# First group's rows of the last eight batches copied inside SBUF by GpSimd's transfers

## The chip, the cores and the metric

The kernel runs on one core of one Trainium2 chip. The metric is the device time of one execution in microseconds (us), as the median of several runs. Everything is in float32. TensorE is called PE below, VectorE DVE, ScalarE ACT, GpSimd POOL and SyncE SP, as the profile calls them. SP and ACT issue transfers on hardware queues (q1 is SP's and q10 ACT's in the profile), and GpSimd on a software queue (q0).

## The reference

Two residual layers act on x of shape (64, 128, 2048): batch, channel, time. The first multiplies each batch by one of 16 matrices, picked by the batch's token. The second is a long convolution along time with a kernel K that is built for each channel from 64 complex exponentials, plus a skip gain D, masked by each batch's length.

```python
x = x + einsum('bct,bcd->bdt', x, W[token])              # W: (16, 128, 128)

dt  = exp(log_dt); A = -exp(log_A_real) + 1j * A_imag    # per channel h, mode n
dtA = A * dt[:, None]
Ct  = (C[..., 0] + 1j * C[..., 1]) * (exp(dtA) - 1) / A
K   = 2 * einsum('hn,hnl->hl', Ct, exp(dtA[:, :, None] * arange(2048))).real
y   = irfft(rfft(x, 4096) * rfft(K, 4096))[..., :2048] + x * D[:, None]
x   = x + y * (arange(2048)[None, :] < length[:, None])[:, None, :]
```

## The kernel before

**Two layers, two layouts.** Time is cut into two segments of 1024 steps. For segment 0 the kernel first does layer one for all 64 batches, one after the other (`batch0(b)`): channels lie on the partitions, the batch's matrix (with the identity added) is the stationary operand, and the result goes back into the loaded tile and from there to a DRAM scratch `scr[0]`. The second layer wants the batches on the partitions: it works on 32 groups of four channels, and `load(i)` fetches group i as a tile `x_i` of 128 rows (64 batches times two halves of the segment), four channels and 512 steps. So the scratch is a transposition between the layers, and `load(0)` can't start until the last batch has been stored.

**A batch of layer one.** `fetch` (L434 to 438) loads two batches, 1 MB, on SP. `weigh` (L440 to 452) lets GpSimd read the token and copy the matrix into one of four buffers `w1`; batch b + 3's is made when batch b is recorded. `project` (L456 to 467) does four matmuls, evicts both PSUM banks into the tile (ACT from batch 18 on) and lets ACT issue the store into the scratch. Batches 12 to 63 are interleaved with the tables of the convolution; the last of these steps, `store_lags`, sends two small transfers `kpad<-krow` from GpSimd at every second batch up to batch 60.

**The seam.** After batch 63 the kernel records `load(0)`, `load(1)` and `some(8)`: the first eight pieces (half batches, two matmuls each) of layer one for segment 1. These need four matrices from GpSimd and the first two of the segment-1 tiles that `fetches(FILL)` asked for at batch 60. Then comes `iteration(-1)`: it loads `x_2`, fetches the fifth segment-1 tile, and for group 0 does the transposes `turn(0, n)`, the input matmuls, and the DVE scan. From then on one iteration per group follows, with pieces of segment 1's layer one between. Here (s, b) is batch b of segment s.

**Order and waits.** Instructions of an engine run in the order in which they were recorded. All tiles `xb` and `x` share one ring of ten buffers (`big`), handed out in the order of the allocations. A transfer is counted on one of eight counters of its kind: one set of eight for the transfers of SP and ACT together, handed out in turn, and another for GpSimd's. A transfer waits until the one that used its counter before has landed, and an engine that waits to issue a transfer does nothing else meanwhile.

Of the kernel before, what the change touches and what calls it, by code (L numbers as in the profile page):

```python
# [41 lines left out]
F32 = mybir.dt.float32  # L42
# [6 lines left out]
P = 128  # L49
# [322 lines left out]
def cond_resid_ssm_kernel(  # L372
# [13 lines left out]
    nc = tc.nc  # L386
    ctx.enter_context(tc.manual_schedule())
    B, C, L = x.shape
# [4 lines left out]
    HL = SL // 2  # L393
    KK = HL // Q
    NQ = 2 * KK
    BK = 512
# [3 lines left out]
    CG = 2 * GP  # L400
# [11 lines left out]
    big = ctx.enter_context(tc.tile_pool(name="big", bufs=10))  # L412
    s0 = ctx.enter_context(tc.tile_pool(name="s0", bufs=4))
    dram = ctx.enter_context(tc.tile_pool(name="dram", bufs=1, space=DRAM))
    psp = ctx.enter_context(tc.tile_pool(name="psp", bufs=1, space=PSUM))

    scr = [dram.tile([P, C, HL], F32, tag=f"scr{s}", name=f"scr{s}") for s in range(NS)]
# [10 lines left out]
    xbs, w1s = {}, {}  # L428
    BT = 2
    QB = SL // BK  # L430
# [3 lines left out]
    def fetch(s, n):  # L434

        xbs[s, n] = big.tile([P, BT, SL], F32, tag="x", name=f"xb_{s}_{n}")
        src = x[n * BT : (n + 1) * BT, :, s * SL : (s + 1) * SL]
        nc.sync.dma_start(xbs[s, n], src.rearrange("b c t -> c b t"))

    def weigh(s, b, plus=None):  # L440

        w1s[s, b] = s0.tile([P, C], F32, tag="w1", name=f"w1_{s}_{b}")
        at = nc.values_load(
            ci[:, b : b + 1],
            engines=(mybir.EngineType.Pool,),
            min_val=0,
            max_val=S - 1,
            skip_runtime_bounds_check_because="it is clamped above",
        )
        w = wres[:, bass.ds(at, 1), :].rearrange("p s d -> p (s d)")  # L450
        if plus is None:
            nc.gpsimd.tensor_copy(w1s[s, b], w)  # L452
        else:
            nc.gpsimd.tensor_tensor(w1s[s, b], w, plus, ALU.add)

    def project(s, b, q, ps, n_banks=1, copy=nc.scalar.copy):  # L456

        n, r = divmod(b, BT)
        own = xbs[s, n][:, r, :]
        for k in range(n_banks):  # L460
            cols = slice((q + k) * BK, (q + k + 1) * BK)
            nc.tensor.matmul(ps[:, k], w1s[s, b], own[:, cols], start=True, stop=True)  # L462
        cols = slice(q * BK, (q + n_banks) * BK)
        copy(own[:, cols], ps.rearrange("p k t -> p (k t)"))  # L464
        if q + n_banks == QB:
            to = scr[s].rearrange("(f b) c t -> b c f t", f=2)[b]
            nc.scalar.dma_start(to, own.rearrange("c (f t) -> c f t", f=2))
            del w1s[s, b]
            if r == BT - 1:
                del xbs[s, n]  # L470

    def batch0(b, copy=nc.scalar.copy):
        if b % BT == 0 and b // BT + AHEAD < B // BT:
            fetch(0, b // BT + AHEAD)
        if b + WAHEAD < B:
            weigh(0, b + WAHEAD)
        project(0, b, 0, psp.tile([P, QB, BK], F32, tag="y", name=f"p0_0_{b}", bufs=2), QB, copy)

    V = nc.vector
    es = [tab.tile([P, TP, 2, NE], F32, tag=f"e{g}", name=f"e_{g}") for g in range(NT)]  # L480
# [4 lines left out]
    def exps(g):  # L485

        for i in range(TP):
            nc.scalar.activation(es[g][:, i, 0, :], steps, AF.Exp, scale=par_of(DRE, g, i))
# [12 lines left out]
    with tc.tile_pool(name="setup", bufs=1) as setup:  # L501
# [87 lines left out]
        for b in range(3):  # L589
            batch0(b)  # L590
        par.sines()
        run(others)
        batch0(3)
        par.lay("ppar_1", rows, 3, par.row(gtab, DRE))
        run(par.gains())
        phases = _weave(par.phases(), masks(), par.steps_of_chunk())
        for b in range(4, 10):
            batch0(b)
            run(phases, 12)
            if b >= 6:  # L600
                exps(b - 6)
# [20 lines left out]
    def partial_angles(k):  # L622

        own = parts[:, :, 0:NL]
        by_l = some_l.unsqueeze(1).to_broadcast([P, NP, NL])

        def of(row, n):
            return gtab[:, row, :].unsqueeze(2).to_broadcast([P, NP, n])

        if k == 0:  # L630
            V.tensor_tensor(own, of(FHI, NL), by_l, ALU.mult)
        elif k == 1:
            V.tensor_scalar(whole, own, MAGIC, MAGIC, ALU.add, ALU.subtract)
        elif k == 2:
            V.tensor_tensor(own, own, whole, ALU.subtract)
        elif k == 3:
            V.tensor_tensor(whole, of(FLO, NL), by_l, ALU.mult)
        elif k == 4:
            V.tensor_tensor(own, own, whole, ALU.add)
        else:  # L640
            V.tensor_tensor(parts[:, :, 0:8], parts[:, :, 0:8], of(PHI, 8), ALU.add)
            V.tensor_tensor(parts[:, :, 24:25], parts[:, :, 24:25], of(PHI, 1), ALU.add)
            V.tensor_scalar(last, parts[:, :, 24:25], MAGIC, MAGIC, ALU.add, ALU.subtract)
            V.tensor_tensor(last, parts[:, :, 24:25], last, ALU.subtract)
# [76 lines left out]
    def some(n):  # L721
        nonlocal done
        for s, b, q in pieces[done : done + n]:
            weights_for(done + WAHEAD * QB + 1)
            project(s, b, q, psp.tile([P, 1, BK], F32, tag="tr", name=f"p0_{s}_{b}_{q}", bufs=2))
            done += 1

    def fetches(n):

        nonlocal begun  # L730
        while begun < min(n + BT * QB, len(pieces)):
            fetch(pieces[begun][0], pieces[begun][1] // BT)
            begun += BT * QB
# [5 lines left out]
            told += QB  # L739

    ps = {}
    FIRST = 18
# [10 lines left out]
        0: turn_parts,  # L755
    }
    for now in range(12, B):
        batch0(now, V.tensor_copy if now < 18 else nc.scalar.copy)
        if now < 20:

            by_row = d_in.rearrange("(h j c d) -> c d j h", j=8, c=2, d=2)
            with nc.allow_non_contiguous_dma(reason="128 gains, four times"):
                for i, r in ((i, r) for i in range(TP) for r in range(4) if (i * 4 + r) // 2 == now - 12):
                    nc.gpsimd.dma_start(dcol[i * NR + r : (i + 1) * NR : 4, :], by_row[r % 2, r // 2])
        if now == 21:
            V.tensor_scalar(dcol, dcol, 1.0, None, ALU.add)
        if now < FIRST:
            partial_angles(now - 12)
        if now < 18:
            exps(2 * now - 20)  # L770
            exps(2 * now - 19)
        for lag, step in STEPS.items():
            g, odd = divmod(now - FIRST - lag, 2)
            if not odd and 0 <= g < NT:
                step(g)
        if now == 60:
            fetches(FILL)
    assert not ps and not ts and not ks
    tmp.__exit__(None, None, None)
    early.__exit__(None, None, None)  # L780


    s1 = ctx.enter_context(tc.tile_pool(name="s1", bufs=2))
    xs, us, ss, bts, tts, ys = {}, {}, {}, {}, {}, {}
    half = [slice(0, B), slice(B, P)]
    NI = NS * NG

    def seg(i):
        return divmod(i, NG)

    def load(i):
        s, g = seg(i)
        xs[i] = big.tile([P, CG, HL], F32, tag="x", name=f"x_{i}")
        nc.sync.dma_start(xs[i], scr[s][:, g * CG : (g + 1) * CG, :])
# [70 lines left out]
    def scan(i, lo, hi):  # L865

        s, g = seg(i)
        st = ss[i]

        def times(row, new, src, own, d):  # L870
            pair = g * GP + d
            factor = ptab[:, row, pair : pair + 1]
            nc.vector.scalar_tensor_tensor(new[:, d, 0:2], src, factor, own[:, d, 0:2], ALU.mult, ALU.add)  # L873

        for m in range(max(lo, 1 if s == 0 else 0), min(hi, NQ if s < NS - 1 else NQ - 1)):
            f, k = divmod(m, KK)
            old, own = st[:, :, :, k, f, :], st[:, :, :, k + 1, f, :]
            new = st[:, :, :, 0, 1, :] if m == KK - 1 else own
            for d in range(GP):
                times(LR, new, old[:, d, 0:2], own, d)  # L880
                if d == 0:
                    nc.vector.tensor_scalar(old[:, :, 2], old[:, :, 0], -1.0, None, ALU.mult)  # L882
            for d in range(GP):
                times(LI, new, old[:, d, 1:3], new, d)
# [49 lines left out]
    def iteration(i):  # L934
# [35 lines left out]
                scan(i + 1, 2, 3) if seg(i + 1)[0] == 0 else scan(i + 1, 1, 2)  # L970
        if nxt:
            scan(i + 1, 3 if seg(i + 1)[0] == 0 else 2, NQ)
    load(0)
    load(1)
    some(8)
    for i in range(-1, NI):
# [33 lines left out]
```

## Time and profile before

| | |
|---|---|
| time, median of 3 runs | 1125.23 us (1122.19 to 1125.81) |
| the profiled execution's own time | 1122.48 us |
| its span | 1120.7 us |
| busy: PE, weight loads, DVE, ACT, POOL | 96%, 70%, 72%, 61%, 22% of the span |
| batches 0 to 63 of segment 0 end on PE at | about 180 us |
| groups of the convolution begin at | 192.1 us |

The page divides the span by engine; the chain of waits gives the work that ended last, from the start to the end; a timeline lists single instructions with their start, their length and, in brackets, how long the engine had idled and for whom. Transfers have two times: what the issuing engine spent, in the timeline, and the time from the issue to the landing, in the list of transfers. About 180 us of 1120 lie before the seam, some 12 us around it; the rest is the loop over the groups, which in its steady part takes 16.55 us a group (the first output matmuls of two consecutive groups start at 217.66 and 234.22 us).

### The profile page before, as it was taken

Reading aid. Unit: us, or ns where it says so; the run is one execution under the profiler, and the core shown is the slowest. Engines: PE = TensorE matmul, PEld = TensorE weight load, DVE = VectorE, ACT = ScalarE, POOL = GpSimd, SP = SyncE. Lnnn points to the kernel's source line nnn. Section 1 sums busy time; section 2 is a strip of 40 time slices with the busy share of each in tenths; the row PEclk is TensorE's granted clock in tenths of the full one; section 3 lists DMA queues with packets and bytes.
Section 4 is the critical chain, followed back from the end, with each engine's and each line's share of the span. In section 5 each row is a group of like instructions: output and inputs, shape, how many; then the busy total and the mean of one; then the engine's idle time right before and its main releaser. Section 6 shows DMA issues by size and latency. Waiting matters only on the chain.

```text
span 1120.7 us, 23853 instructions
## 1 busy us (share of the span) xinstructions
PE 1076.6 (96%) x8634; PEld 786.6 (70%) x8634; DVE 803.0 (72%) x2671; ACT 680.7 (61%) x1123; POOL 242.5 (22%) x421
## 2 busy tenths in 40 slices
PE   5779998999999999999999999999999999999996
PEld 2224443677777777777777778888888888888885
DVE  7656550467657667667666758888888888888886
ACT  3577665766666566566566566665566566556652
POOL 3253332121221212122122211211211111121110
PEclk9899999999999999999999999999999999999999
DMA  9999999999999999999999887787787887788754
GB/s 346 415 398 386 409 410 379 357 281 285 344 280 294 298 293 298 302 299 281 293 299 284 260 264 212 225 228 226 229 228 210 237 230 223 216 240 228 210 166 118
DMA packets 117126, 313.25 MB, mean 280 GB/s; under 512 B 11858, under 2 KB 11986, under 8 KB 108818
## 3 DMA queue, kind: packets, MB, share of 16 engines
q1 hardware_dynamic: 70928, 218.65, 62.1%
q10 hardware_dynamic: 35106, 67.64, 16.1%
q0 software_dynamic: 10976, 25.45, 8.9%
q8 instruction: 68, 1.11, 0.4%
q14 instruction: 48, 0.39, 0.1%
HBM read 164.76 MB, written 146.93 MB: 278 GB/s over the span
## 4 chain that ended last, share of the span: by engine, by line
PE 91%; DMA 3%; DVE 2%; ACT 1%; issue 1%; ACTq 0%; SPq 0%; POOLq 0%; DVEq 0%
PE y L911 21%; PE y L899 20%; PE v L858 18%; PE p L462 17%; PE tr L833 10%; DMA xb<-in_x_dram 2%; PE pb L815 2%; PE pt L660 1%; DMA scr<-xb 1%; PE pk L690 1%; DVE s L873 1%; DMA x<-scr 1%; ACT xb L464 0%; DVE xb L464 0%; DVE x L920 0%
## 5 line engine op out<-in xcount | busy, mean ns | idle before, releaser
L873 DVE SCALAR_TENSOR_TENSOR s<-s,ptab 128x128 f32<-128x128 f32 x1792 | 520.2, 343 | 109.0 <-ACT s L863 92.7
L863 ACT ACTIVATE s<-v,ptab 64x512 f32<-64x512 f32 (+1 forms) x512 | 336.0, 656 | 50.4 <-PE v L858 33.9
L899 PEld LDWEIGHTS y<-tt,u 128*128 128x128 f32 x2048 | 263.5, 192 | 80.5 <-issue 67.0
L462 PE MATMUL p<-xb,w 128*128 128x512 f32 x512 | 257.9, 617 | 22.4 <-DMA xb<-in_x_dram 10.9
L899 PE MATMUL y<-tt,u 128*128 128x128 f32 x2048 | 269.9, 275 | 0.1
L911 PEld LDWEIGHTS y<-e,s 64*128 64x128 f32 x4096 | 233.9, 188 | 46.6 <-issue 24.2
L858 PE MATMUL v<-u,bt 128*128 128x512 f32 (+1 forms) x512 | 248.6, 567 | 0.0
L911 PE MATMUL y<-e,s 64*128 64x128 f32 x4096 | 246.7, 275 | 1.4 <-DVE s L873 1.4
L834 ACT COPY u<-tr 128x512 f32<-128x512 f32 x256 | 150.5, 588 | 156.6 <-PE tr L833 130.2
L882 DVE TENSOR_SCALAR s<-s 128x128 f32<-128x128 f32 x448 | 98.8, 221 | 137.6 <-ACT s L863 137.6
L464 ACT COPY xb<-p 128x512 f32<-128x512 f32 (+1 forms) x186 | 133.4, 718 | 83.9 <-PE p L462 80.7
L920 DVE COPY_PREDICATED x<-mask,y 128x1024 f32<-128x1024 uint8 x128 | 166.5, 1301 | 1.1 <-PE y L911 1.0
L833 PEld LDWEIGHTS tr<-ident,x 128*128 128x128 f32 x1024 | 121.6, 141 | 54.8 <-issue 49.3
L833 PE MATMUL tr<-ident,x 128*128 128x128 f32 x1024 | 156.3, 275 | 3.9 <-DMA x<-scr 3.9
L462 PEld LDWEIGHTS p<-xb,w 128*128 128x128 f32 x512 | 87.9, 197 | 89.3 <-issue 80.1
L452 POOL COPY w<-wres 128x128 f32 x125 | 58.6, 469 | 291.7 <-PE p L462 291.3
L801 POOL DMA_DIRECT2D tt<-kpad x64 | 50.5, 789 | 207.3 <-DVE s L873 168.0
L858 PEld LDWEIGHTS v<-u,bt 128*128 128x128 f32 x512 | 79.9, 192 | 13.9 <-issue 13.6
L846 POOL DMA_DIRECT2D s<-carry x64 | 44.9, 706 | 126.1 <-PE y L911 121.4
L816 ACT COPY bt<-pb 128x512 f32<-128x512 f32 x32 | 18.8, 586 | 87.5 <-PE pb L815 86.7
L890 POOL DMA_DIRECT2D carry<-s x64 | 43.6, 721 | 69.7 <-DVE s L873 63.6
L843 POOL MEMSET s<- 128x384 f32 x32 | 14.8, 462 | 149.4 <-DMA carry<-s 66.6
(199 smaller groups left out, 296.1 us busy)
## 6 DMA issues: line engine op xcount, KB each, us to landing
xb<-in_x_dram SPq DMA_DIRECT2D x64, 1024.0 KB, 10.1
scr<-xb ACTq DMA_DIRECT2D x128, 512.0 KB, 8.3
x<-scr SPq DMA_DIRECT2D x64, 1024.0 KB, 8.1
out_dram<-x SPq DMA_DIRECT2D x126, 512.0 KB, 4.8
tt<-kpad POOLq DMA_DIRECT2D x64, 256.0 KB, 5.9
btd<-bt SPq DMA_DIRECT2D x32, 256.0 KB, 7.2
bt<-btd SPq DMA_DIRECT2D x32, 256.0 KB, 4.9
carry<-s POOLq DMA_DIRECT2D x64, 64.0 KB, 7.1
```

The costliest lines, as they stand in the source:

```text
L452: nc.gpsimd.tensor_copy(w1s[s, b], w)
L462: nc.tensor.matmul(ps[:, k], w1s[s, b], own[:, cols], start=True, stop=True)
L464: copy(own[:, cols], ps.rearrange("p k t -> p (k t)"))
L833: nc.tensor.transpose(tr[:, k, :], xs[i][:, c, k * Q : (k + 1) * Q], ident)
L834: nc.scalar.copy(u, tr)
L858: nc.tensor.matmul(v[:, 0:nv], w, us[i, n].rearrange("p k r -> p (k r)")[:, 0:nv], start=True, stop=True)
L863: nc.scalar.activation(own[:, 0:nv], v[lanes, 0:nv], AF.Copy, scale=amp)
L873: nc.vector.scalar_tensor_tensor(new[:, d, 0:2], src, factor, own[:, d, 0:2], ALU.mult, ALU.add)
L882: nc.vector.tensor_scalar(old[:, :, 2], old[:, :, 0], -1.0, None, ALU.mult)
L899: nc.tensor.matmul(y[:, k, :], u[:, k, :], tts[i][:, n, :], start=(k == 0), stop=False, skip_group_check=True)
L911: nc.tensor.matmul(ys[i, d][:, c, k, :], st[half[c], d, part, k, :, :].rearrange("p f b -> p (f b)"), e[half[c], pair % TP, part, 0:Q], st ...
L920: nc.vector.copy_predicated(xs[i][:, d::2, :].rearrange("r c (k t) -> r c k t", k=KK), keep_k.unsqueeze(1).to_broadcast([P, 2, KK, Q]), ys ...
```

## The change

The tile `x_0` is now allocated at batch 56, before the fetches of segment 1. Each of the batches 56 to 63, once its eviction is recorded and its store issued, has two more transfers on GpSimd (`own_rows`): the first four partitions of the batch's tile, one half of the segment each, go straight to the batch's row of `x_0` (one partition, 8 KB). The rows of batches 0 to 55 are loaded from the scratch by two transfers on SP (`early_rows`), recorded right after batch 63 where the program goes on to `load(1)`. `load(0)` is gone. That is sixteen more transfers on GpSimd's queue, and two of 56 rows on SP in place of one of 128.

```diff
-    def project(s, b, q, ps, n_banks=1, copy=nc.scalar.copy):
+    def project(s, b, q, ps, n_banks=1, copy=nc.scalar.copy, then=None):
...
             nc.scalar.dma_start(to, own.rearrange("c (f t) -> c f t", f=2))
+            if then is not None:
+                then(b)
             del w1s[s, b]
...
-    def batch0(b, copy=nc.scalar.copy):
+    def batch0(b, copy=nc.scalar.copy, then=None):
...
+    EARLY = 56
+    xs = {}
+
+    def own_rows(b):
+        own = xbs[0, b // BT][0:CG, b % BT, :]
+        for f in range(2):
+            r = f * B + b
+            nc.gpsimd.dma_start(xs[0][r : r + 1].rearrange("o c t -> o (c t)"), own[:, f * HL : (f + 1) * HL])
+
+    def early_rows():
+        for f in (0, B):
+            nc.sync.dma_start(xs[0][f : f + EARLY], scr[0][f : f + EARLY, 0:CG, :])
...
     for now in range(12, B):
-        batch0(now, V.tensor_copy if now < 18 else nc.scalar.copy)
+        if now == EARLY:
+            xs[0] = big.tile([P, CG, HL], F32, tag="x", name="x_0")
+        batch0(now, V.tensor_copy if now < 18 else nc.scalar.copy, own_rows if now >= EARLY else None)
...
         if now == 60:
             fetches(FILL)
+        if now == B - 1:
+            early_rows()
...
-    load(0)
     load(1)
     some(8)
```

More of the change, by code (lines that the diff above doesn't have):

```diff
@@ L476, in batch0 @@
             weigh(0, b + WAHEAD)
-        project(0, b, 0, psp.tile([P, QB, BK], F32, tag="y", name=f"p0_0_{b}", bufs=2), QB, copy)
+        project(0, b, 0, psp.tile([P, QB, BK], F32, tag="y", name=f"p0_0_{b}", bufs=2), QB, copy, then)
     V = nc.vector
@@ L783, in cond_resid_ssm_kernel @@
     s1 = ctx.enter_context(tc.tile_pool(name="s1", bufs=2))
-    xs, us, ss, bts, tts, ys = {}, {}, {}, {}, {}, {}
+    us, ss, bts, tts, ys = {}, {}, {}, {}, {}
     half = [slice(0, B), slice(B, P)]
```

## The prediction

> **What bounds the kernel now.** I read the page first, then the chain of waits, then the timeline around the seam, then the windows there, then the transfers.
>
> ```profile
> PE 1076.6 (96%) x8634; PEld 786.6 (70%) x8634; DVE 803.0 (72%) x2671; ACT 680.7 (61%) x1123; POOL 242.5 (22%) x421
> ...
> PE 91%; DMA 3%; DVE 2%; ACT 1%; issue 1%; ACTq 0%; SPq 0%; POOLq 0%; DVEq 0%
> ...
> 165.90 15.66 PE p L462 x36
> 182.05 3.79 PE p L462 x8
> 186.19 5.79 DMA x<-scr
> 192.12 0.92 PE tr L833 x4
> ```
>
> PE carries the time nearly everywhere. The change can win only at the seam, where the chain leaves PE: x_0 is loaded from 186.19, when the last store has landed, to 192.1, and PE has run out of other work at 188.2.
>
> ```profile
> 179.87 1.01 ACT L464 COPY xb<-p 128x1024 f32<-128x1024 f32 x1 [0.70 <-PE p L462]
> 180.91 0.37 ACTq L467 DMA_DIRECT2D scr<-xb  x1
> 187.58 0.64 PE L815 MATMUL pb<-ident,e 128*128 128x128 f32 x4
> 192.12 0.92 PE L833 MATMUL tr<-ident,x 128*128 128x128 f32 x4 [3.90 <-DMA x<-scr]
> ...
> 190.00:192.00 2.00, 0.00 (x0) 0.00 (x0) 0.00 (x0) 0.00 (x0) 0.00 (x0) 1.00 0.99 391
> 192.00:194.00 2.00, 1.88 (x6) 1.29 (x7) 0.00 (x0) 0.59 (x1) 0.00 (x0) 0.58 1.04 318
> 194.00:196.00 2.00, 2.00 (x7) 1.20 (x6) 0.00 (x0) 0.94 (x2) 0.00 (x0) 0.57 0.97 381
> 196.00:198.00 2.00, 2.00 (x9) 1.15 (x8) 0.00 (x0) 1.59 (x3) 0.29 (x1) 1.00 1.06 441
> ```
>
> Columns of the last four rows: stretch, length, busy time of PE, weight loads, DVE, ACT, POOL, then granted clock, DMA share, GB/s. Batch 63 ends on PE at 179.87 (its eviction starts there). The eight pieces run to 187.55, the four transposes pb to 188.2, PE idles 3.9 us, and then the granted clock is 0.57 to 0.58 from 192 to 196: about 4 x 0.43 = 1.7 us lost, say 1.6. **The most to win is 3.9 + 1.6 = 5.5 us.**
>
> **What the change removes.** load(0) leaves the end of the stage. The two early transfers have old stores to wait for (below) and the rows of 56 to 63 need no DRAM. If nothing else moved, PE would go from pb straight to the transposes: minus 5.5 us.
>
> **What it adds on GpSimd.** Sixteen issues, and GpSimd also makes the matrices. The nearest row is the other four-descriptor transfer; its time to land is in the list of transfers from 150 to 200 us:
>
> ```profile
> 173.10 0.30 POOL L452 COPY w<-wres 128x128 f32 x1 [1.42 <-PE p L462]
> 173.60 1.00 POOL L710 DMA_DIRECT2D kpad<-krow  x2 [0.20 <-issue]
> 175.13 0.30 POOL L452 COPY w<-wres 128x128 f32 x1 [0.53 <-PE p L462]
> ...
> kpad<-krow POOLq DMA_DIRECT2D x12, 2.0 KB, 5.1
> ```
>
> So 0.5 us an issue, about 0.55 us a matrix with its gap, 5.1 us to land (extremes 4.5 and 8.6). A pair of batches takes PE 2 x 1.72 = 3.44 us; GpSimd now needs 4 x 0.5 + 1.0 + 2 x 0.55 = 4.1 us. Over the span it is 22% busy; here it becomes the slower one. Order on its queue: matrix b + 3, two rows of b, kpad if b is even. The rows of 56 wait for that eviction, 168.9, and everything is behind them:
> - rows 56 to 169.9, kpad 170.9, matrix 60 at 171.5 (PE wants it at 173.0); rows 57 172.6, matrix 61 173.1 (174.7); rows 58 174.2, kpad 175.2, matrix 62 175.7 (176.4); rows 59 176.8, matrix 63 177.3 (178.15). All in time by 0.7 us or more: the batches themselves lose nothing.
> - From here the eight counters bite. Rows 60 reuse those of rows 57 (landed 176.7): 177.4 to 178.4. kpad of 60 reuses rows 58: 179.4. Rows 61 reuse kpad of 58: 180.4. Rows 62 reuse rows 59, landed 180.9 and 181.4: done 181.9. Rows 63 reuse rows 60, landed 182.5 and 183.0: done 183.5. The matrix of (1, 0) stands behind all of them: 183.75 to 184.05.
>
> Before, that matrix was copied at 175.13. **PE therefore idles from 179.87 to about 184.3, 4.4 us**, where it ran on. The pieces then take 7.7 us and pb 0.65, and PE reaches the transposes near 193 without a wait: rows 63 land at 183.0 + 5.1 = 188.1, the early rows by about 187.
>
> Two rules of the Trainium skill bear here. *DMA: Bandwidth & Descriptors*, "Anatomy of one DMA — SWDGE (gpsimd) path", fits a GpSimd transfer as some 2.0 us plus its bytes over 436 GB/s. By that hardly a counter would be waited for: rows 61 end at 180.4, rows 62 at 181.4, rows 63 at 182.4, the matrix is there at 182.95, and the hole is 3.1 us. The row says 5.1 us with the engines saturated (405 GB/s in this stretch), so I take 5.1; 7 us instead would put the matrix at about 187. *TensorE: Matmul & The Clock Gate*, Part 1, says that the clock falls after an idle window of about 3.4 us. The rows agree (3.9 us idle, then 0.58), and it speaks against the change: the cold stretch isn't saved, it moves with the hole. At 4.4 us I charge it again, 1.2 us (the pieces have 0.8 us of slack); at 3.1 us it would be nothing.
>
> Sum on PE: +4.4 (new hole) + 1.2 (cold there) - 3.9 - 1.6 (old hole, old cold) + 0.5 (the eviction of pb was hidden in the old hole, not now) = **+0.6 us**, between -1.8 (landing 3 us or less, clock kept) and +3.8 (landing 7 us).
>
> **What it moves on SP and ACT.** x_0 takes the ring's buffer of batches 44 and 45 at batch 56, so the four segment-1 fetches, held by each buffer's stores and by their new counters, come one tile or more later. In the built program they wait for stores 49, 51, 53, 55: about 158, 165, 170 and 174 us, where the trace has 149.5, 156.5, 160.5 and 166. The first is wanted at 180: harmless alone. But the transfer engines lose work between 150 and 164 (2.5 MB of loads before, 1 MB now) and have 1.5 MB more afterwards, plus the early rows' 0.9 MB, which wait by their counters for stores 56 and 57, about 176: 2.4 MB at 0.405 MB/us is 6 us. The stores (8 us to land before 170, 5.3 for the last) share with that, while PE's hole takes away about 1 MB of stores. I put the last store's landing at 188.5 (187 to 191) instead of 186.2. load(1), load(2) and the fifth segment-1 fetch stand behind it on SP, in that order.
>
> That would be covered (x_1 is wanted near 205), but for the counters: the store of (1, 4), ACT's at
>
> ```profile
> 198.65 0.37 ACTq L467 DMA_DIRECT2D scr<-xb  x1
> ...
> x<-scr SPq DMA_DIRECT2D x1, 1024.0 KB, 5.8
> ...
> xb<-in_x_dram SPq DMA_DIRECT2D x1, 1024.0 KB, 15.1
> ```
>
> waited for x_1 before (landed 196.1) and now waits for that fifth fetch. Before, x_0 landed 5.8 us after its issue, x_1 and x_2 each 4.05 us behind, and the fetch (issued 188.61, 15.1 us) at 203.7, 3.5 us behind x_2. With x_0 out of the queue: 188.5 + 5.8 + 4.1 + 3.6 = 202.0. ACT, busy 3.92 of 4.00 us between 200 and 204, stands still until then, with the evictions of the transposes and the DVE scan behind it. So the end moves by 202.0 - 198.65 = **+3.3 us** (between 0, if the last store isn't later, and +6), in place of the 0.6, not on top of it: the later of the two chains decides. Nothing after it gives the time back, because the loop is PE's at 16.55 us a group.
>
> Costed at nothing: the GpSimd rows' bandwidth (16 x 8 KB), and two loads of 56 rows for one of 128. Store 62 on ACT now waits for store 58 (about 178.5, wanted 179.2): nothing, and up to 1.5 us is hidden behind rows 60.
>
> **Rivals.**
> - *Only the hole on GpSimd counts* (+0.6): the last store lands as before. For it: DMA share falls to 0.88 at 184 to 186, so there is a reserve. Against it: the same bytes are due later. 1125.8.
> - *It wins, on the other side*: rows land in about 2 us, an issue costs less than 0.3 us, and matrix (1, 0) is there by about 181; then PE keeps its clock and goes warm into the transposes, up to -5.5: 1119.7. It decides when the new hole is under about 1.5 us. Against it: the 0.5 us and 5.1 us rows, and that rows 63 can't be issued before the eviction at 180.9.
> - *Congestion*: GpSimd's transfers take 7 us or more, ACT is held at store 62, the last store lands at 192: +7, 1132.2.
> - *It doesn't do what it says*: the early rows wait for late stores after all. The built program excludes it: they wait for 54, 56 and 57.
>
> **The numbers.** The profiled execution took 1122.48 (span 1120.7 and 1.8 around it), 2.75 under the median 1125.23, as fast as the fastest run; so I carry the difference over to the median. Held store: 1125.23 + 3.3 = 1128.5, chance 0.45, its own spread 1126 to 1131. Only the hole: 0.32, 1123.4 to 1128. Congestion: 0.15. Win: 0.08. 0.3% is 3.4 us, about what a measurement of this kernel can tell from no change (its three runs spread by 3.6). The likeliest case straddles it: a bit under two thirds of it, some 0.29, and all of congestion are slower, with a few hundredths of the second: 0.47. Same 0.46, faster 0.07. Range 1123.0 to 1132.5.
>
> **What would show it.** In the profile after: POOL busy nearly without a gap from 169 to 184, matrix (1, 0) near 184 and not 175; PE idle 4 us just before the first piece and none before the first transpose of x_0; the granted clock low near 184 to 188 and 1.00 at 192 to 196; the ACT store of (1, 4), the fifth after the stage, near 202 with ACT idle ahead of it, released by the xb load. Wrong if matrix (1, 0) comes before 182, if batches 60 to 63 themselves wait for matrices, or if the store of (1, 4) follows its eviction at once.

## The result: 1% slower, and the profile after

The changed kernel takes 1136.88 us (median of 5 runs, 1133.98 to 1139.03), the kernel before 1125.23 beside it (1121.82 to 1125.81). The ratio is 1.0111, 95% interval 1.0087 to 1.0135: 11.65 us slower, where 1128.5 was forecast and 1132.5 was the upper end of the range. The profiled execution took 1139.03 us, the slowest of the five; its span is 1136.8, 16.1 over the span before. All of that arises at the seam: the first `y<-e,s` matmul (the output of group 0) starts at 217.59 us before and at 232.92 after, 15.3 us later, and no later stage gives it back.

The page after, busy time of the engines and then the chain by engine:

```profile
PE 1081.2 (95%) x8634; PEld 788.5 (69%) x8634; DVE 802.4 (71%) x2671; ACT 680.0 (60%) x1123; POOL 250.9 (22%) x437
...
PE 88%; DMA 8%; DVE 1%; ACT 1%; issue 0%; ACTq 0%; SPq 0%; DVEq 0%
```

PE has the same 8634 instructions and is 4.6 us longer busy: matmuls at a low clock. The other 11.5 us of the 16.1 are idle time. Transfers have 8% of the chain instead of 3%. The chain of waits at the seam (start, length, what):

```profile
173.17 9.79 DMA scr<-xb
...
184.49 13.23 DMA scr<-xb
...
199.43 13.67 DMA xb<-in_x_dram
...
213.18 0.37 ACTq L467
...
213.58 0.59 ACT u L854
...
214.22 1.11 PE tr L853 x4
```

It leaves PE at 172 and comes back only at 214. In between stand three transfers: the store of batch 58, on whose landing ACT's issue of the store of batch 62 waited; the store of batch 63, on which SP's loads waited; and the fifth segment-1 fetch, on which the store of (1, 4) waited. The timeline of PE shows where that is paid (start, length, instructions; in brackets how long PE had idled, and for whom):

```profile
177.91 1.98 PE L462 MATMUL p<-xb,w 128*128 128x512 f32 x4 [0.67 <-POOL w L452]
180.09 1.98 PE L462 MATMUL p<-xb,w 128*128 128x512 f32 x4 [0.19 <-POOL w L452]
191.35 9.19 PE L462 MATMUL p<-xb,w 128*128 128x512 f32 x16 [9.28 <-POOL w L452]
...
201.21 0.66 PE L853 MATMUL tr<-ident,x 128*128 128x128 f32 x4
...
214.22 1.11 PE L853 MATMUL tr<-ident,x 128*128 128x128 f32 x4 [6.00 <-ACT u L854]
```

The wait for x_0, 3.90 us before, is gone: the transposes at 201.21 follow without one. In its place PE waits 9.28 us for the matrix of (1, 0), which GpSimd makes, and 6.00 us for ACT, which stands at the store of (1, 4). GpSimd's and ACT's timelines hold the two reasons:

```profile
170.00 1.00 POOL L751 DMA_DIRECT2D x<-xb  x2 [3.37 <-DMA scr<-xb]
...
176.01 1.00 POOL L712 DMA_DIRECT2D kpad<-krow  x2 [1.01 <-DMA x<-xb]
...
184.18 0.50 POOL L751 DMA_DIRECT2D x<-xb  x1 [1.91 <-DMA kpad<-krow]
185.47 0.51 POOL L751 DMA_DIRECT2D x<-xb  x1 [0.79 <-DMA kpad<-krow]
188.50 1.00 POOL L751 DMA_DIRECT2D x<-xb  x2 [2.52 <-issue]
190.00 1.00 POOL L751 DMA_DIRECT2D x<-xb  x2 [0.50 <-DMA x<-xb]
191.00 0.30 POOL L452 COPY w<-wres 128x128 f32 x1
```

```profile
183.04 0.37 ACTq L467 DMA_DIRECT2D scr<-xb  x1
183.45 1.01 ACT L464 COPY xb<-p 128x1024 f32<-128x1024 f32 x1 [2.50 <-DMA scr<-xb]
184.49 0.37 ACTq L467 DMA_DIRECT2D scr<-xb  x1
...
213.18 0.37 ACTq L467 DMA_DIRECT2D scr<-xb  x1
213.58 0.58 ACT L854 COPY u<-tr 128x512 f32<-128x512 f32 x1 [6.60 <-DMA xb<-in_x_dram]
```

From 176 on GpSimd stops at its own counters: the kpad pair of batch 58 for rows 56, rows 61 for that kpad pair, rows 62 for rows 59 and rows 63 for rows 60 (the timeline names no releaser for 188.50; rows 59 had landed at 187.97 and 188.69). The rows that it issued between 178 and 186 took long to land:

```profile
DMA to landing us min/median/max: 7.3/9.3/10.1
```

The kpad pair of 176.01 took 7.6 and 8.7 us; the kpad row of before has 5.1. The windows (stretch, length, busy time of PE, weight loads, DVE, ACT, POOL, then granted clock, DMA share, GB/s), the first line of the kernel before, the others of the changed one:

```profile
150.00:164.00 14.00, 14.00 (x77) 5.92 (x76) 8.21 (x17) 9.68 (x17) 5.29 (x12) 1.00 1.04 410
...
150.00:164.00 14.00, 14.00 (x77) 5.89 (x76) 8.08 (x17) 10.18 (x16) 5.30 (x12) 1.00 0.89 305
...
184.00:188.00 4.00, 0.00 (x0) 0.00 (x0) 0.00 (x0) 0.46 (x1) 1.01 (x2) 0.55 1.04 364
188.00:192.00 4.00, 0.65 (x1) 0.50 (x2) 0.00 (x0) 0.00 (x0) 2.36 (x6) 0.50 0.95 313
192.00:196.00 4.00, 4.00 (x7) 1.45 (x6) 0.00 (x0) 1.17 (x2) 1.11 (x4) 0.67 0.39 148
```

Two things are to be seen: the transfers that are missing early (305 GB/s from 150 to 164, 410 before), because the segment-1 fetches wait for their ring buffers, and the clock, which is 0.50 to 0.55 from 184 on and still low when PE starts again at 191.35.

### The profile page after: what moved, and what is told of

The parts are those of the page before. It is cut to its first block, busy times and chain, and to the rows that moved or that the text cites. A ratio compares the mean times of both kernels' runs of the same rounds, so it can differ in the third digit from the quotient of the medians.

```text
span 1136.8 us, 23896 instructions
## 1 busy us (share of the span) xinstructions
PE 1081.2 (95%) x8634; PEld 788.5 (69%) x8634; DVE 802.4 (71%) x2671; ACT 680.0 (60%) x1123; POOL 250.9 (22%) x437
## 4 chain that ended last, share of the span: by engine, by line
PE 88%; DMA 8%; DVE 1%; ACT 1%; issue 0%; ACTq 0%; SPq 0%; DVEq 0%
PE y L931 21%; PE y L919 20%; PE v L878 18%; PE p L462 15%; PE tr L853 10%; DMA xb<-in_x_dram 5%; DMA scr<-xb 4%; PE pb L835 2%; PE pt L662 1%; PE pk L692 1%; DVE s L893 1%; DVE x L940 0%; ACT xb L464 0%; ACTq L467 0%; ACT e L490 0%
```

## The experiments

Three theories were put against each other; the expectations use their letters. **A**: the ring shift makes fetches late, transfers pile up at the end of the stage, the last store and with it the fifth fetch land late, and the held store of (1, 4) sets the end. **B**: GpSimd's queue alone sets it, by the late matrix of (1, 0). **C**: loads of 56 (and 8) rows spread badly over the transfer engines and hold the stores. The kernel before ran with each set: 1125.11, 1125.43, 1125.29 and 1124.73 us. All times are medians; a ratio is to the kernel before, with its 95% interval (it is not the quotient of the two medians and differs from it by up to 0.14%). A trace is of one execution: those of e1 (1129.49 us) and e4 (1129.03) were the fastest of their five, that of the changed kernel the slowest.

| kernel | what it is | us | ratio | first `y<-e,s` at |
|---|---|---|---|---|
| before | | 1125.23 | | 217.59 |
| after | | 1136.88 | 1.0111 (1.0087 to 1.0135) | 232.92 |
| e1 | after, fetches ahead of x_0 | 1131.48 | 1.0062 (1.0044 to 1.0081) | 224.19 |
| e2 | after, no GpSimd rows, no ring shift | 1129.83 | 1.0040 (1.0023 to 1.0056) | 226.95 |
| e3 | after, matrices ahead of rows | 1136.60 | 1.0093 (1.0066 to 1.0120) | 233.02 |
| e4 | after, store of (1, 4) on SP | 1132.76 | 1.0069 (1.0040 to 1.0097) | 223.71 |
| e5 | before with the ring shift | 1129.05 | 1.0030 (1.0016 to 1.0044) | 225.77 |
| e6 | before, x_0 loaded as 56 + 8 rows | 1128.52 | 1.0026 (1.0012 to 1.0040) | 224.31 |
| e7 | before, x_0 loaded as 48 + 16 rows | 1127.71 | 1.0013 (0.9995 to 1.0031) | 221.41 |
| e8 | before, twelve pieces | 1120.21 | 0.9947 (0.9929 to 0.9966) | 213.16 |
| e9 | e1 and e3 together | 1133.72 | 1.0089 (1.0059 to 1.0119) | 227.98 |
| e10 | e1, e3 and e4 together | 1127.14 | 1.0019 (1.0005 to 1.0033) | 222.41 |
| e11 | e10 and twelve pieces | 1126.23 | 1.0019 (1.0004 to 1.0035) | 220.45 |
| e12 | before, sixteen pieces | 1121.27 | 0.9972 (0.9957 to 0.9988) | 216.85 |
| e13 | ring shift and early loads, no GpSimd rows | 1128.27 | 1.0034 (1.0019 to 1.0049) | 222.41 |
| e14 | ring shift and GpSimd rows, no early loads | 1129.38 | 1.0043 (1.0025 to 1.0061) | 224.95 |
| e15 | GpSimd rows alone | 1131.62 | 1.0055 (1.0040 to 1.0070) | 227.58 |

**e1: the fetches of segment 1 come before x_0 takes its buffer.**

```diff
         if now == EARLY:
+            fetches(FILL)
             xs[0] = big.tile([P, CG, HL], F32, tag="x", name="x_0")
...
-        if now == 60:
-            fetches(FILL)
```

> The change with one thing put back: the four segment-1 fetches are recorded ahead of x_0's allocation, so they take the buffers that they had before and x_0 takes that of batches 52 and 53. Theory A (the late fetches pile up the transfers, and the held store of (1, 4) sets the end): the fetches are issued at about 150 to 166 us again, the last store of segment 0 lands before 190 instead of 197.7, the GpSimd hole shrinks from 9.3 to about 5 us since its transfers land sooner, the store of (1, 4) goes out near 202: some 8 to 10 us better than the change, 1127 to 1129. Theory B (the sixteen transfers on GpSimd's queue set the end by themselves): the hole stays at 8 us or more and the time at 1134 to 1137. Theory C (the two loads of 56 rows lag on a few transfer engines and hold the stores): the last store still lands after 194; 1133 or more.

Measured: 1131.48, 5.4 us under the changed kernel, between A's 1127 to 1129 and B's 1134 to 1137. From 150 to 164 the transfers run at 407 GB/s again. The last store lands at 190.3 instead of 197.7, the store of (1, 4) goes at 205.25 instead of 213.18. The hole before the pieces is still there, third line of PE's timeline:

```profile
174.75 3.78 PE L462 MATMUL p<-xb,w 128*128 128x512 f32 x8 [2.46 <-POOL w L452]
179.09 3.79 PE L462 MATMUL p<-xb,w 128*128 128x512 f32 x8 [0.55 <-POOL w L452]
189.06 9.66 PE L462 MATMUL p<-xb,w 128*128 128x512 f32 x16 [6.19 <-POOL w L452]
```

The ring shift thus carries about half of the loss, and B's hole remains with 6.2 us. The 2.46 us are new: x_0 now takes a younger buffer, and GpSimd's first rows wait for that buffer's stores and go out at 171.84.

**e2: no rows by GpSimd.** x_0 is first written after the fetches are recorded, so these keep their buffers; the last eight rows of each half are loaded at the end.

```diff
-        batch0(now, ..., own_rows if now >= EARLY else None)
+        batch0(now, ...)
...
+    for f in (0, B):
+        nc.sync.dma_start(xs[0][f + EARLY : f + B], scr[0][f + EARLY : f + B, 0:CG, :])
     load(1)
```

> The change without GpSimd's copies: rows 56 to 63 of both halves come from the scratch by two more transfers on SP once the last store has landed, rows 0 to 55 as in the change; x_0 is first written at batch 63, so the fetches of segment 1 have their old buffers too. Theories A and B: no hole before the first piece, fetches at their old times; the last store lands near 187 and 0.13 MB follow in about 3 us, so PE gets x_0 near 190 instead of 192.1: 1122 to 1126, the time of before or a little better. Theory C: the two loads of 56 rows still hold the last stores to 192 or later and the time is 1129 or more.

Measured: 1129.83. Without GpSimd's rows and without the shift there is still a loss of 4.7 us, so neither A nor B tells all of it. PE waits for x_0 longer than before:

```profile
179.00 7.11 PE L462 MATMUL p<-xb,w 128*128 128x512 f32 x16 [1.88 <-ACT xb L464]
...
200.55 1.09 PE L853 MATMUL tr<-ident,x 128*128 128x128 f32 x4 [7.78 <-DMA x<-scr]
```

The early loads take their bandwidth while the stores need it: the last store lands at 193.3 (186.0 before), and the 0.13 MB that remain to be loaded take 7 us. This spoke for C.

**e3: matrices of batches 0 to 2 of segment 1 ahead of GpSimd's rows.**

```diff
         if b + WAHEAD < B:
             weigh(0, b + WAHEAD)
+        else:
+            weigh(1, b + WAHEAD - B)
```

> The change with the matrices of (1, 0) to (1, 2) made with batches 61 to 63, ahead of these batches' rows on GpSimd's queue. Theory B: the 9.3 us hole is gone and the seam moves to where rows 63 land, about 195 instead of 201: 1130 or so, 6 us better. Theory A: the hole goes, but the store of (1, 4) still waits for the fifth fetch, landed at 213, and that alone sets the end: within 1.5 us of the change, 1135 to 1137.

Measured: 1136.60, the changed kernel's time, as A has it. PE's 9.28 us break up into 1.75, 0.47 and 4.47 us. The timeline gives the 4.47 to GpSimd's matrices, but the matrix of (1, 2) was copied at 190.40 and PE starts at 192.93, when ACT has emptied a PSUM bank: ACT stood at the store of (1, 0), whose counter waited for the store of batch 60. ACT's timeline:

```profile
191.84 0.37 ACTq L467 DMA_DIRECT2D scr<-xb  x1
192.25 1.07 ACT L464 COPY xb<-p 128x512 f32<-128x512 f32 x2 [5.40 <-DMA scr<-xb]
```

So PE reaches the transposes at 201.92, no earlier than before the edit (201.21), and ACT stands again until 213.54: PE waits 5.66 us there, and the first `y<-e,s` comes at 233.02 against 232.92. While these stores are late, taking matrices out of GpSimd's queue brings nothing; what the hole costs alone this run doesn't tell.

**e4: SP issues the store of (1, 4).**

```diff
-            nc.scalar.dma_start(to, ...)
+            queue = nc.sync if (s, b) == (1, 4) else nc.scalar
+            queue.dma_start(to, ...)
```

> The change with one store, that of (1, 4), issued by SP instead of ACT: the same wait for the fifth fetch, but with nothing of PE's work behind it. Theory A (the held ACT queue at 208 to 213 us sets the end): PE's second hole of 6 us closes to about 1 us and the time falls by 4 to 6 us, to 1131 to 1133. Theory B (only the hole at 182 to 191 counts and the rest is slack): no more than 1 us better, 1136.

Measured: 1132.76, 4.1 us under the changed kernel, as A has it. One store of 0.5 MB on another engine, nothing else moved, and PE's wait of 6.00 us is gone from the trace. The intervals of the two kernels just overlap (the runs of e4 spread from 1129.03 to 1136.87), so the size of some 4 us is rough; that the held store costs time is shown beyond the noise by e10. What remains is the hole, 6.76 us here. Up to this store e4 and the changed kernel are the same program, so the difference of that hole from 9.28 shows how far two executions differ.

**e5: only the ring shift.**

```diff
+        if now == 56:
+            xs[0] = big.tile([P, CG, HL], F32, tag="x", name="x_0")
+            V.memset(xs[0][0:1, 0, 0:1], 0.0)
```

> The kernel before, with one thing of the change alone: x_0 is allocated at batch 56 (one element of it is written there), so that it takes the buffer of batches 44 and 45 and the fetches of segment 1 come one ring place later. GpSimd carries no rows, and load(0) reads all 128 rows at the end as before. Theory A (late fetches pile up transfers at the end of the stage and hold stores and the fifth fetch): the stretch 150 to 164 falls to about 0.9 of the DMA engines, the last store lands 4 us or more after 186.2, first y<-e 4 to 8 us after 217.6, time 1129 to 1133. Theory B (GpSimd's queue alone sets the end): nothing of the queue is in here, so the time is the kernel before's within 1.5 us, 1124 to 1127. Theory C (loads of 56 rows hold the stores): nothing of those is in here either, so 1124 to 1127.

Measured: 1129.05, +3.6 us, by A's lower end. No row moves, no instruction is added but one memset; only four fetches come one place later. The transfers fall to 374 GB/s from 150 to 164, the last store lands at 190.5 (186.0 before), and the load of x_0, issued at 190.66, takes 8.62 us (5.79):

```profile
190.00 0.64 PE L820 MATMUL pb<-ident,e 128*128 128x128 f32 x4
199.41 1.09 PE L838 MATMUL tr<-ident,x 128*128 128x128 f32 x4 [8.78 <-DMA x<-scr]
```

**e6 and e7: x_0 in four loads at the place of one**, 56 and 8 rows of each half, or 48 and 16.

```diff
-        nc.sync.dma_start(xs[i], scr[s][:, g * CG : (g + 1) * CG, :])
+            for lo, hi in ((0, 56), (56, B)):
+                for f in (0, B):
+                    nc.sync.dma_start(xs[i][f + lo : f + hi], scr[s][f + lo : f + hi, 0:CG, :])
```

> The kernel before, with x_0 loaded at the same place by four transfers in place of one: rows 0 to 55 of both halves, then rows 56 to 63 of both. Same bytes, same waits. Theory C (transfers of 56 and of 8 rows are spread unevenly over the transfer engines): x_0 lands 3 us or more later than the 5.8 us of before, PE idles 7 us or more where it idled 3.9, time 1127 to 1130. Theory A or B: three more issues on SP, 0.4 us each, 1.2 us at most: PE idles 4 to 5 us, time 1125 to 1127.

> As the run with 56 and 8 rows, with 48 and 16 in place of them. Theory C, if it is the number of rows that spreads badly: 48 and 16 go evenly over 16 engines, so x_0 lands 5.8 to 7 us after the last store and the time is 1125 to 1127, 2 us or more below the run with 56 and 8. Without C both runs agree within 1 us.

Measured: 1128.52 and 1127.71, 0.8 us apart and with intervals that overlap, where C wanted 2 us or more. The loads of the large parts don't wait for the last store, so they were issued at 177.0 and 171.3, among the stores, as in the changed kernel: it was an early load again, and in e7 some 6 us earlier than in e6, so the pair doesn't compare the numbers of rows alone. After the last store the small parts took 6.00 us (8 rows) and 6.87 us (16 rows), against 5.79 for all 128 rows before: for these the number of rows matters little.

For the large parts C's premise holds, though not its price. The packed trace keeps, beside what the views print, when each of the sixteen parts of a store landed. In e6 two parts of the store of batch 63 landed at 187.2 and 187.3, the other fourteen from 189.5 to 192.1; in e7 all sixteen from 187.4 to 188.6. Such a lead of two parts, up to 3 us among the last four stores, is in every kernel with an early load of 56 rows; without one it is at most 0.3 us. It looks as if 56 rows went over fourteen of the sixteen transfer engines and delayed the stores there (the trace names no engine). What this uneven spread costs beyond the early load itself is not separated.

What is shown is the price of an early load, 3.1 us in e6 and 2.3 in e7 (not clear of the noise): the last store lands at 192.1 (184.28 + 7.80) and 188.6, because the loads share with it and ACT is held once by a counter:

```profile
177.82 7.10 PE L462 MATMUL p<-xb,w 128*128 128x512 f32 x16 [1.43 <-ACT xb L464]
...
199.13 1.09 PE L838 MATMUL tr<-ident,x 128*128 128x128 f32 x4 [7.53 <-DMA x<-scr]
```

Those are e6's. In stretches in which x_0 is read the transfers move 310 GB/s (e6, 180 to 184) and 317 (e7, 172 to 180) at a share of about 1, and 303 at 0.96 in the kernel before (186 to 190), where stores alone move 405 (176 to 180): reading x_0 is slow early and late. Early, it slows the stores.

**e9 and e10: what is left when the causes found are mended.** e9 joins e1's and e3's edits, e10 adds e4's.

> The changed kernel with two things mended at once: the fetches of segment 1 recorded ahead of x_0's allocation (they keep their buffers, as in e1), and the matrices of batches 0 to 2 of segment 1 weighed ahead of GpSimd's rows (as in e3). By theory A the ring shift is the main cost and GpSimd's hole the next one, and the held store of (1, 4) no longer decides once the fetch is early: the 6.2 us hole of e1 shrinks to 2 us or less, time 1126 to 1129, 2.5 us or more under e1. By theory C (loads of x_0 that run beside the stores slow them, wherever GpSimd stands) the stores stay late and the time stays within 1.5 us of e1, 1130 to 1133. By theory B alone it falls to that of the kernel before, 1125.

> As e9, with the store of (1, 4) issued by SP besides, so that ACT isn't held by it. By theory A, in which the fifth fetch is early enough now, this adds nothing: within 1 us of e9. If ACT is still held in e9 until that fetch lands, 2 us or more under it, and the change at its best: 1122 to 1126.

Measured: 1133.72 and 1127.14. e9 is a miss: not below e1. GpSimd's holes shrink to 2.09 us at the longest, as was expected, but the fifth fetch, issued at 193.61, takes 14.84 us, and ACT stands for it. Timelines of ACT and of PE in e9:

```profile
208.93 0.58 ACT L856 COPY u<-tr 128x512 f32<-128x512 f32 x1 [7.99 <-DMA xb<-in_x_dram]
```

```profile
209.56 1.11 PE L855 MATMUL tr<-ident,x 128*128 128x128 f32 x4 [7.38 <-ACT u L856]
```

The time won at GpSimd is lost at the held store, the mirror image of e3. Moved to SP (e10) that store costs nothing, 6.6 us less, though not the 1122 to 1126 hoped for. With all three mended the change is 1.9 us slower than the kernel before: GpSimd still makes PE wait 4.7 us in four places, more than the 3.9 us that the wait for x_0 was.

**e8, e11, e12: fill the wait in place of moving the load.** `some(8)` becomes `some(12)` (e8) and `some(16)` (e12) in the kernel before; e11 is e10 with `some(12)`.

> The kernel before, with twelve pieces of segment 1 in place of eight ahead of the first transposes (some(12)), so that PE has work through the 3.9 us in which it waits for x_0 and its clock doesn't fall. What the prediction called the most to win, 5.5 us: 1120 to 1123 if the pieces fill the wait and the later stages, with four pieces fewer to fill, lose nothing. If the fifth fetch, which twelve pieces need earlier, isn't there in time, or the pieces are missing later: 1125 to 1127.

> As e10, with twelve pieces in place of eight ahead of the first transposes. If rows that come early are worth something beside a filled wait, it is under e8 (1120.2): 1116 to 1119. If the wait for x_0 was all there was to win, and the pieces have won it, the rows only cost: 1121 to 1125, above e8.

> The kernel before with sixteen pieces in place of eight. If e8's gain is the filled wait of PE, which twelve pieces fill already, four more win nothing, and what they take from later stages may show: 1120 to 1123. If it is something else that grows with the pieces (matrices or fetches that come earlier), it goes on falling: 1115 to 1118.

Measured: e8 1120.21, 5.2 us under the kernel before; this beats both kernels, by one number. Its PE timeline and one window:

```profile
181.59 9.44 PE L462 MATMUL p<-xb,w 128*128 128x512 f32 x20 [0.50 <-POOL w L452]
190.87 0.64 PE L815 MATMUL pb<-ident,e 128*128 128x128 f32 x4
191.79 0.63 PE L833 MATMUL tr<-ident,x 128*128 128x128 f32 x4 [0.28 <-ACT xb L464]
```

```profile
192.00:194.00 2.00, 1.35 (x9) 0.89 (x8) 0.00 (x0) 1.32 (x3) 0.64 (x2) 1.00 1.02 418
```

The 3.9 us are filled and the granted clock is 1.00 where it was 0.58: the prediction's 5.5 us "most to win" could be won nearly whole, without a transfer being moved. Sixteen pieces win no more (1121.27): ACT is held twice then, 1.08 and 2.13 us, by loads of x tiles. e11 lies above both of its ranges and isn't better than the kernel before: with the wait filled the rows bring nothing, and GpSimd's 5.0 us of waits stay.

**e13, e14, e15: which pair makes the long stores.** e13 has early loads and the shift, rows 56 to 63 loaded at the end as in e2. e14 has GpSimd's rows and the shift, and x_0 is zeroed once in place of the early loads. e15 is e14 with e1's order of the fetches. Both leave out most of x_0, so they price time alone.

```diff
 # e13
+            V.memset(xs[0][0:1, 0, 0:1], 0.0)
-        batch0(now, ..., own_rows if now >= EARLY else None)
+        batch0(now, ...)
 # e14, e15
+            V.memset(xs[0], 0.0)
...
-        if now == B - 1:
-            early_rows()
```

> The changed kernel without GpSimd's transfers, but with its ring order: one element of x_0 is written at batch 56, so the fetches of segment 1 come late as in the change, rows 0 to 55 of each half are loaded early on SP, rows 56 to 63 by two transfers on SP at the end. In the changed kernel the last stores took 13 to 17 us to land; with the ring shift alone (e5) 6 to 9, with early loads but no shift (e2) 7 to 10. If the late fetches and the early loads together pile up (theory A in its new form), the last stores take 12 us or more here too, time 1131 to 1136. If it needs GpSimd's queue beside them, they take 7 to 10 us and the time is that of e2 and e5, 1128 to 1131.

> The changed kernel without the early loads: rows 0 to 55 of each half of x_0 are zeros written once at batch 56 by VectorE and never loaded, so 0.9 MB of transfers is left out. Late fetches and GpSimd's rows are in. If the long stores come from fetches and early loads together, they take 6 to 9 us here and only GpSimd's hole is left, 5 to 9 us, with no wait for x_0: 1124 to 1128. If they come from GpSimd's rows beside the late fetches, 12 us or more, 1130 to 1135.

> As e14, with the fetches of segment 1 recorded ahead of x_0's allocation: GpSimd's rows are the only part of the change left, and 0.9 MB of loads is left out. Theory B's own price, which the prediction put at a hole of 4.4 us against the 3.9 us wait that goes: hole 4 to 6 us, stores land in 4 to 7 us as before, time 1123 to 1127. If the hole is as in e1 or more (6.2 us and up) although the loads are gone, GpSimd's queue is slow by itself: 1126 to 1130.

Measured: 1128.27, 1129.38, 1131.62: e13 as expected without GpSimd, e14 between its two cases. The store of batch 63 in one execution of each, from its issue to its landing:

| kernel | shift | early loads | GpSimd rows | issued at | us to land |
|---|---|---|---|---|---|
| before | | | | 180.91 | 5.1 |
| e5 | x | | | 183.33 | 7.2 |
| e2 | | x | | 185.46 | 7.9 |
| e13 | x | x | | 181.19 | 8.6 |
| e14 | x | | x | 184.77 | 7.4 |
| e1 | | x | x | 183.95 | 6.3 |
| after | x | x | x | 184.49 | 13.2 |
| e3 | x | x | x | 184.56 | 13.9 |
| e4 | x | x | x | 185.53 | 9.0 |

None of the three pairs has the long stores; only kernels with all three parts do (in e4 those of batches 60 and 61 have them, 14.6 to 15.1 us, where the pairs have at most 10.1; its last one has 9.0). The times are less plain. The pairs cost 3.5 us (shift and loads), 4.65 (shift and rows) and 6.4 (loads and rows, e1), the three together 11.65; but alone the parts cost 3.6 (e5), 4.7 (e2) and 6.9 (e15, with a wait of its own), which is 15.2. So the prices don't add. e14 holds GpSimd's price with the change's ring order:

```profile
171.28 1.00 POOL L751 DMA_DIRECT2D x<-xb  x2 [3.40 <-DMA scr<-xb]
...
188.42 1.00 POOL L751 DMA_DIRECT2D x<-xb  x2 [1.82 <-DMA x<-xb]
```

```profile
189.95 9.47 PE L462 MATMUL p<-xb,w 128*128 128x512 f32 x16 [6.26 <-POOL w L452]
```

The rows for whose counters others wait land in 5.3 to 6.1 us here, close to the 5.1 of the prediction, and still the hole is 6.26 us. The changed kernel's 9.28 (6.76 in e4) are this and 0.5 to 3 us of longer landings. e15, with rows alone, is a miss on the high side. In its order of buffers GpSimd's first rows wait 8.76 us for old stores, matrices come late for the batches themselves (4.37 us on PE, then 2.88), so it prices that wait more than the rows.

## Why the prediction was wrong

Sign and mechanisms held; the sizes did not, and one assumption about how they add up failed.

| step of the prediction | predicted | measured |
|---|---|---|
| segment-1 fetches issued, first and last | 158, 174 | 158.4, 177.5 |
| GpSimd's transfers to land, those for which others wait | 5.1 us | 7.6 to 10.1 |
| matrix of (1, 0) starts | 183.75 | 191.00 |
| hole on PE before the pieces | 4.4 us | 9.28 |
| last store lands | 188.5 | 197.7 |
| fifth fetch lands, store of (1, 4) goes | 202.0 | 213.1, 213.18 |
| PE's wait for x_0 | none | none |
| end moves by | +3.3 | +11.65 |

*The step that set the time is the landing of the last store, 188.5.* By the prediction's own sum the store of (1, 4) goes 13.5 us after it (5.8 + 4.1 + 3.6). Measured are 15.5 us (197.7 to 213.18), so 9.2 of the 11.2 us by which that store came later than forecast lie in this one term. The ring shift in it was priced well: alone it lands the last store at 190.5, within the 187 to 191 given, and costs 3.6 us, almost the +3.3 of the forecast. But that is nearly the whole forecast for one of three parts. Early loads were costed as 0.9 MB at the usual rate; e6 shows 3.1 us for loading early, and e13 stores of 8 to 10 us. The list of transfers by queue (packets, MB, share of the engines; q1 is SP's, q10 ACT's), from 177 to 185 before and then from 181 to 190 after, shows what the sum missed:

```profile
q10 hardware_dynamic: 1676, 3.23, 104.1%
...
q1 hardware_dynamic: 396, 1.88, 57.2%
q10 hardware_dynamic: 634, 1.22, 41.6%
```

Before, the last stores have the transfer engines to themselves, 0.40 MB/us. After, the last segment-1 fetch (issued at 177.51) and the early rows (179.29 and 180.61, not about 176) come in one block of 1.9 MB beside them, and the stores move 0.14 MB/us until it is through.

*The second is the landing of a GpSimd transfer, 5.1 us, as a constant.* It was read off the kpad transfers of the kernel before (which took 4.5 to 6.3 us; the 8.6 given there as their extreme is that of a `tt<-kpad` of 256 KB) and put into a queue of eight counters, where every microsecond of landing comes back once a round. In the changed kernel it is 7.6 to 10.1 us. The prediction's own "7 us instead would put the matrix at about 187" pointed at the danger, and its price went into a rival with a chance of 0.15. The Trainium skill's fit (*DMA: Bandwidth & Descriptors*, "Anatomy of one DMA — SWDGE (gpsimd) path", 2.0 us and the bytes) lay further off still; the trace's row was the better one to take, and too low. And e14 shows that the schedule was 1.9 us short even at 5.3 to 6.1 us: rows 56 were put at 168.9, but the eviction of batch 56, for which they wait, ended at 170.98 there and at 169.70 in the changed kernel, and they went out 0.3 us behind it, at 171.28 and 170.00 (the timeline names a store that landed just before); rows 63 went out at 188.4 where 182.5 was written.

*The third is "the later of the two chains decides".* That is true of the two waits in one trace (e9, which mends one and wins nothing, e10, which mends both), but the chains were sized apart, as if they didn't share the transfer engines and ACT. ACT's store of batch 62 waited for that of batch 58 until 183.04, which the prediction costed at nothing with 1.5 us in reserve; it held the eviction of batch 63 for 2.5 us and the issue of the last store until 184.49 (180.91 before). GpSimd's last rows were held not by this but by their own counters. The two chains lengthened together: of the transfers issued from 176 to 186, ACT's took 13.2 to 16.8 us and GpSimd's 7.3 to 10.1.

*What was right*: the order on GpSimd and the counters as the thing that bites; that the wait for x_0 goes and a new one for the matrix of (1, 0) comes; that the store of (1, 4) is held by the fifth fetch (shown by e4 and e10); that the early rows aren't tied to late stores; that the cold clock moves with the hole instead of going. Also wrong, but small: batches 60 to 63 lost 0.67 and 0.19 us to late matrices where nothing was put. Of the rivals, congestion is the one that came: rows over 7 us, ACT held at store 62, the last store later than its 192. It was drawn as a separate accident; it came in all three kernels traced that have the change's three parts.

## What to carry to other kernels

In this case a landing time followed the load on the transfer engines more than the transfer (one 8 KB row took 1.9 to 10.1 us): before putting such a time into a schedule with a few counters, ask what the change adds to that load, and price the schedule at twice the landing too. A load moved earlier leaves the end only if nothing that still has to finish shares its path; here it slowed the last stores, and in e2 and e6 its own last rows had to wait for these. And where an engine idles for a transfer, first look for work that can be put there: one number (twelve pieces for eight) won 5.2 us where moving the load lost 11.65.

## What the runs showed of the hardware that was not expected

- A transfer can be out for long while the engines are nearly idle. In the changed kernel the store of batch 63 (0.5 MB) is out until 197.7, and in the last stretch but one the share is 0.15 (columns as above):

```profile
192.00:194.00 2.00, 2.00 (x3) 0.68 (x2) 0.00 (x0) 0.54 (x1) 0.82 (x3) 0.50 0.64 240
194.00:196.00 2.00, 2.00 (x5) 0.78 (x4) 0.00 (x0) 0.63 (x2) 0.29 (x1) 0.83 0.15 56
```

  One part of sixteen is late: of this store, fifteen parts had landed by 195.4 and the last at 197.7. For the last four stores this lag is 1.3 to 2.6 us in the changed kernel, 1.7 to 3.0 in e3, 1.6 to 1.9 in e4, 1.3 to 1.4 in e2 and e6, about 0.5 before, and at most 0.7 in the rest but for one store of e15 (1.4). The trace names no engine for a part, so it stays open which one lags and why, as does why the longest stores take all three parts of the change.
- The landing of the last load hardly depends on its size: 5.79 us for 1 MB (before), 6.00 for 0.13 MB (e6), 6.87 for 0.26 MB (e7), each with 1 MB loads right behind it (e6 and e7: the later of two halves).
- GpSimd's row copies of 8 KB, the same instruction in the same place of the code, took 1.9 to 2.2 us to land when issued at 181.0 and 181.5 in e15, where the share fell to 0.05 (182 to 184), 5.2 to 5.5 us when issued at 176.5 and 177.0 there, at 1.05 (176 to 178), and up to 10.1 us in the changed kernel. The 2.0 us of the Trainium skill's fit, cited above, were met only where the engines were nearly idle.
- The granted clock fell to 0.58 after 3.9 us of idle PE in the kernel before and to 0.50 in the longer holes; in e8, whose longest wait there is under a microsecond, it stayed at 1.00.
